# Two attention layers on eight images: layer 1's weighted sum by seven block products for six images, squares on two queues, steps ordered anew

## The chip, the cores and the metric

The kernel runs on one core of a Trainium2 chip. A core has TensorE (PE, with its weight loads shown as PEld), VectorE (DVE), ScalarE (ACT), GpSimd (POOL) and the queue engine SyncE (SP). Each engine works through its own queue in order. The metric is the device time in microseconds, the median of three runs.

## The reference

The input x is 8 images of 32 x 32 positions with 256 channels, all float32. So an image has 1024 tokens. Layer 0 is attention with four heads, layer 1 a gated attention with 32-wide keys.

```python
# layer 0, for each image b and head h
qkv = x @ W_qkv                      # q, k, v of 256 channels a head
atten = softmax(q @ k.T * 256**-0.5)
res = atten @ v
x1 = concat(res over heads) @ W_out + b_out + x

# layer 1
f, g, h = x1 @ Wf + bf, x1 @ Wg + bg, x1 @ Wh + bh
b = softmax(g @ f.T)                 # over the tokens of f
out = gamma * (b @ h) + x1
```

The softmax is over 1024 tokens. The division by the sum of exponentials can stand after the product with the values, because the sum belongs to the row of the output.

## The kernel before

**Steps.** The program is a list of steps. In layer 0 a step is one image, one head and one of two blocks of 512 query tokens. In layer 1 a step is one image and one block. For images 1 to 6 the list holds, in this order, heads 0 and 1 of the image, both blocks of layer 1 of the image before, and then heads 2 and 3. I name the steps of such an image 00, 01, 10, 11 (head, block), l0, l1, 20, 21, 30, 31. In the last image layer 1 of image 6 comes after all heads, and layer 1 of image 7 forms the end.

**What a step issues.** The loop over the steps at the end of the program collects tasks of several steps: the scores of this step, the block sums and value products of the step before, the last third of those products, the output projection and the queries of the next head. Each task gets a number (`put(tasks, *at)`), and the tasks are issued in the order of these numbers. TensorE, VectorE and ScalarE keep exactly this order (`manual_schedule`); the queues of SyncE and GpSimd are ordered by the framework.

**Seven products.** Large products are done on 2 x 2 blocks with seven products in place of eight (`seven`, line 253, `product` on line 271, whose matmuls all stand on line 273). One operand needs four sums of blocks beforehand (`sum_a`, `sum_b`). The function gives three tasks. Task one runs products 1 and 6, task two runs 5, 7 and 2, and task three runs 3 and 4; between them ScalarE copies partial results out of PSUM and VectorE adds them (line 290). Product 6 is the first that needs two dependent sums of blocks. Score banks are named psz, psy, psx; those of the value product have `_y`, of the output projection `_o`, of the queries `_q`.

**Layer 0.** Exponentials p (line 600) of a step are 128 x 8 x 512. The step after makes the block sums of p (line 638, tile ss), adds up all exponentials over the tokens in the free direction (lines 645 and 649, tile rs), and GpSimd adds over the partitions (PARTITION_ALL_REDUCE, line 651). The row of sums goes through DRAM to become columns (tile st), is inverted (line 667) and spread again over all partitions (tile invb). VectorE multiplies the projected output by it (line 725), and GpSimd's queue adds it to x1T by an accumulating DMA (line 728). The sums of the queries (tile qs) are on line 579.

**Layer 1.** f and g are made in one 128-row product and moved to four row groups (`queries_apart`, lines 804 and 816). The scores run four at a time on 32 rows (line 845), and ScalarE writes their exponentials (line 854, tile s). `values` makes gamma * (x1 @ Wh + bh) with 16 matmuls (line 518) and VectorE's line 828. `row_products` then runs, for each block, 4 x 8 matmuls of 257 columns (line 933, tile pa; column 257 is one, so it gives the sum of the exponentials), a reciprocal of it (line 941), and one instruction that multiplies and adds to x1 (line 943).

**Transposes.** x and x1 are turned between token rows and channel rows by DMAs of 32 x 32 squares and VectorE transposes within squares (`squares`, line 396, and line 418). All these DMAs are on SyncE's queue: 224 for x0T and 256 for x1.

Of the kernel before, what the change touches and what calls it, by code (L numbers as in the profile page):

```python
# [20 lines left out]
def kernel(  # L21
# [67 lines left out]
    FAR = 2.0**64  # L89
# [289 lines left out]
    xT_of, x1T_of, xblocks, vblocks = {}, {}, {}, {}  # L379
# [16 lines left out]
    def squares(dst, src, swap):  # L396

        Q = 32  # L400

        def move(a, c):
            for q in range(P // Q):
                to, rows_v = dst(), src()
                if swap:
                    nc.sync.dma_start(
                        to[ts(q, Q), :, c, ts(a, Q)], rows_v[ts(a, Q), c, :, ts(q, Q)]
                    )
                else:
                    nc.sync.dma_start(  # L410
                        to[ts(q, Q), c, :, ts(a, Q)], rows_v[ts(a, Q), :, c, ts(q, Q)]
                    )

        def piece(k):
            to = dst()
            n = to.shape[1] * to.shape[2] // 4
            flat = to.rearrange("p u v i -> p (u v) i")[:, ts(k, n), :]
            nc.vector.transpose(flat, flat)

        return (  # L420
            [partial(move, a, c) for a in range(P // Q) for c in range(CC)],
            [partial(piece, k) for k in range(4)],
        )
# [37 lines left out]
    def value_sums(b):  # L461

        made = {}

        def piece(i):
            if i == 0:
                r = rows[b]
                t = tile_of("xt", [P, 4, NT // 2, P], f"xt_{b}")
                blocks = [r[:, ts(j, NT // 2), ts(c, P)] for j in range(2) for c in range(CC)]
                sums = [t[:, k] for k in range(4)]  # L470
                made["l"] = sum_b(sums, *blocks)
                vblocks[b] = b_operands(blocks, sums)
            made["l"][i]()

        return [partial(piece, i) for i in range(4)]
# [58 lines left out]


    class Layer0:
# [82 lines left out]
        def sums(self, blk):  # L619
# [4 lines left out]
            made = {}  # L624

            def start():
                half = NT // 2
                p = self.p[blk]
                blocks = [p[:, ts(j, half), ts(e, HB)] for e in range(2) for j in range(2)]
                t = tile_of("ss", [P, 2, half, HB], f"ss_{n}")  # L630
                sums = [t[:, 1], t[:, 0], blocks[2], t[:, 0]]
                self.pblocks[blk] = a_operands(blocks, sums)
                made["t"], made["l"] = t, sum_a(sums, *blocks)

            def piece(i):
                if i == 0:
                    start()
                made["l"][i]()
# [8 lines left out]
            def last():  # L647
                r = made["r"]
                tt(r[:, 0, :], r[:, 0, :], r[:, 1, :], ALU.add)
                self.total[blk] = t = tile_of("rb", [P, NB], f"rb_{n}")  # L650
                nc.gpsimd.partition_all_reduce(  # L651
                    t, r.rearrange("p e i -> p (e i)"), P, bass_isa.ReduceOp.add
                )
                line = tile_of("line", [1, NB], f"line_{n}")
                nc.sync.dma_start(line, t[0:1, :])
                self.r[blk] = st = tile_of("st", [P, HT], f"st_{n}")
                with nc.allow_non_contiguous_dma(reason="a row of sums turns into columns"):
                    nc.sync.dma_start(st, line.rearrange("o (p t) -> p (o t)", p=P))

            adds = [partial(add, k) for k in range(1, NT // 2)]  # L660
            return [partial(piece, i) for i in range(4)], adds + [last]

        def invert(self, blk):
# [4 lines left out]
            if blk in self.rb:  # L668
                return
            line = tile_of("line", [1, NB], f"inv_{self.name}_{blk}")  # L670
            with nc.allow_non_contiguous_dma(reason="columns turn into a row"):
                nc.sync.dma_start(line.rearrange("o (p t) -> p (o t)", p=P), inv)
            self.rb[blk] = t = tile_of("invb", [P, NB], f"invb_{self.name}_{blk}")
            nc.sync.dma_start(t, line[0].partition_broadcast(P))
# [6 lines left out]
        def products(self, blk):  # L681


            def out(c, e):
                if blk not in self.y:
                    self.y[blk] = tile_of("y", [P, CC, NB], f"y_{self.name}_{blk}")
                return self.y[blk][:, c, ts(e, HB)].unsqueeze(1)

            return seven(
                f"y_{self.name}_{blk}", HB, 1,  # L690
                lambda number: [
                    (0, vblocks[self.b][number][:, j, :], self.pblocks[blk][number][:, j, :])
                    for j in range(NT // 2)
                ],
                {
                    "11": partial(out, 0, 0), "12": partial(out, 1, 0),
                    "21": partial(out, 0, 1), "22": partial(out, 1, 1),
                },
                NARROW,
            )  # L700
# [42 lines left out]
    class Layer1:  # L743
        scale = 1.0

        def __init__(self, b, direct=0):

            self.b, self.name, self.direct = b, f"{b}_l1", direct
            self.s = {}
            self.fg, self.v = None, None  # L750

# [23 lines left out]
        def queries_apart(self, tag=None):  # L775
# [7 lines left out]
            def task():  # L783
                fg = self.fg_tile()
                self.f, self.g = fg[:, 0, :], fg[:, 1, :]
                if tag is None:
# [33 lines left out]
        def values(self, last="psm"):  # L820
            def start():
                if self.v is None:
# [5 lines left out]
                lambda t2, pm: nc.vector.scalar_tensor_tensor(  # L828
                    self.v[:, 2 * t2 : 2 * t2 + 2, :C], pm, gamma_sb,
                    bh_sb.unsqueeze(1).broadcast_to([P, 2, C]), ALU.mult, ALU.add,  # L830
# [40 lines left out]
        def products(self, blk):  # L871
            return row_products(self, blk, rows1)

# [118 lines left out]
    steps, adds, exps = [], {}, {}  # L992

    for b in range(B):
        units = [Layer0(b, h) for h in range(HEADS)]
        if b > 0:
            units.insert(behind(b), Layer1(b - 1, NBLK))
        steps += [(u, blk) for u in units for blk in range(NBLK)]
# [9 lines left out]
    first_sums = value_sums(0)  # L1008
# [10 lines left out]
    for i, (a, blk) in enumerate(steps):  # L1019
        l0 = isinstance(a, Layer0)  # L1020
        one, two, nxt = step(i - 1), step(i - 2), step(i + 1)
        places = []

        def put(tasks, *at):
# [3 lines left out]
        if l0:  # L1028
            tasks, exps[i] = a.scores(blk)
            put(tasks, 0, 2, 4, 6, 8, 10)  # L1030
            put(exps[i][:2], 5.1, 6.1)
        else:
            tasks, _ = a.scores(blk)
            put(tasks, *((0.5, 2.4) if blk == 0 else (0.5, 2)))
        if is_l0(two):
            u, k = two
            put(u.products_of[k][2:], 1 if l0 else 0)
            if nxt is None:
                put([partial(u.invert_all, k)], 2.2)
            put([partial(u.invert, k)], 3.4 if l0 else 2.7)  # L1040
            ysums, tasks, adds[i] = u.project(k)
            put(ysums, *((1.1, 1.2, 1.3, 3.3) if l0 else (1.1, 1.2, 1.3, 2.5) if blk == 0 else
                         (0.6, 0.7, 0.8, 0.9)))
            put(tasks, *((3, 5.5, 7) if l0 else (4.5, 6, 7.2) if blk == 0 else
                         (3, 5, 7) if nxt else (1.9, 3.1, 4.1)))
            if nxt is None:
                put(adds[i], 4.2)
        if i - 1 in exps:
            put(exps[i - 1][2:], *((0.9, 0.91) if l0 else (0.1, 0.2)))
        if i - 1 in adds:  # L1050
            put(adds[i - 1], 0.5 if l0 or blk == 1 else 2.3)
        if is_l0(one):
            u, k = one
            sums, keys = u.sums(k)
            u.products_of[k] = u.products(k)
            put(sums, *((2.1, 3.2 if is_l0(two) else 2.4, 4.2, 5.6) if l0 else (0.8, 2.2, 3.5, 6.1)))
            put(keys, *((6.3, 6.6, 7.6, 8.7) if l0 else (6.3, 7.6, 8.3, 8.7)))
            put(u.products_of[k][:2], *((5, 9) if l0 else (4, 5)))
        elif one is not None:
            put(one[0].products(one[1]), *((3, 5, 7, 9) if l0 else (1, 4, 6, 8) if nxt else (1, 3, 4, 8.5)))  # L1060
        if i == 0:
            put(fold[0], 3.1, 3.2, 6.4, 6.5, 8.6)
            put(first_sums[:2], 8.4, 9.4)
        if i == 1:
            put(first_sums[2:], 1.4, 3.4)
            put(fold[1], 0.5, 0.6, 2.4, 2.6, 5.6)
            put(fold[2], 7.2, 7.3, 7.9, 9.2, 9.5)
            put([partial(nc.vector.tensor_scalar, bh_sb, bh_sb, gamma_sb, None, ALU.mult)], 8.5)

        if l0 and blk == 0:  # L1070
            put(a.query_sums(1), 3.5, 4.3, 4.4, 5.3)
        if is_l0(nxt) and blk == NBLK - 1:
            put(nxt[0].queries(), *((2.5, 4.5, 6.5) if not l0 else
                                    (1.5, 2.5, 4.5) if is_l0(two) else (0.5, 2.5, 5.5)))
            put(nxt[0].query_sums(0), *((6.7, 6.9, 7.3, 7.6) if not l0 else
                                        (5.4, 6.4, 7.2, 7.4) if is_l0(two) else (6.4, 7.2, 7.3, 7.4)))

        if l0 and a.h == 0 and blk == 1:
            put(residual(a.b), 5.3, 7.3)
        if l0 and a.h == 0 and blk == 1 and a.b > 0:  # L1080
            put(value_sums(a.b), 1.4, 2.4, 3.4, 4.4)
        if l0 and a.h == 1 and blk == 0 and a.b + 1 < B:
            load_x(a.b + 1)
        if is_l0(nxt) and nxt[0].h == 2 and nxt[1] == 0 and nxt[0].b + 1 < B:
            moves, turned = turn_rows(nxt[0].b + 1)
            put(moves[:4], 1, 2.5, 4, 5.5)
        if l0 and a.h == 2 and a.b + 1 < B:
            if blk == 0:
                put(moves[4:], 0.5, 1.5, 2.5, 3.5)
                put(turned, 6.4, 7.4, 8.4, 9.4)  # L1090
            else:
                put(key_sums(a.b + 1), 0.5, 0.6, 6.4, 7.4)

        if l0 and a.b > 0 and a.h == behind(a.b) - 1:
            if blk == 0:
                moves, turned1 = turn_back(a.b - 1)
                put(moves[:4], 3, 4.5, 6, 7.5)
            else:
                put(moves[4:], 4, 5.5, 7, 8.5)
                tasks, moves = nxt[0].queries_apart()  # L1100
                put(tasks, 1.5)
                put(moves, 1.6, 1.7, 1.8, 1.9)
        if not l0 and blk == 0:
            put(a.values("ps"), 0.9, 1, 2.3, 3, 6.5)
            put(turned1, 2.5, 2.9, 4.2, 5.1)
# [152 lines left out]
```

## Time and profile before

| | |
|---|---|
| median of 3 runs | 2305.72 us (2305.56 to 2306.0) |
| profiled execution | 2305.9 us, span of its instructions 2304.0 us |
| TensorE busy | 2293.2 us |
| VectorE busy | 1508.4 us |
| ScalarE busy | 756.9 us |
| GpSimd busy | 340.9 us |
| granted TensorE clock | 1.000 |

The profile is of one execution. A group is a line of the program with its engine, operation, tiles (output <- inputs), shape and count; then busy microseconds, mean nanoseconds of one, and the idle time of the engine just before. In the waits, a line says who waited for whom, in microseconds in total, how often, and the longest. In a timeline, the first number is the start in microseconds from the start of the span, the second is the duration; neighbouring equal instructions are merged (x4 means four). Matmul ends are modelled, so two neighbours overlap in the record, and the distance of starts is the real pace. A float32 matmul instruction shows as two records.

### The profile page before, as it was taken

To read this page: it belongs to the slowest core of one execution; us is meant where nothing else is said; L and a number is where in the kernel's file an instruction comes from. 1 tells how busy PE (TensorE), PEld (TensorE's weight loads), DVE (VectorE), ACT (ScalarE), POOL (GpSimd) and SP (SyncE) were. 2 spreads that over 40 slices of the span, in tenths; PEclk is the share of its full clock that TensorE was granted. 3 is DMA by queue.
4 is the path that set the end of the run, shared out by engine and by line. 5 is a ranking of instruction groups with operands and counts; after the bars stand their busy time and mean duration, and the time that the engine had idled before them with its cause. 6 is when DMAs were issued, how large, how long until landed. Compare 5 with 4: busy or idle time off the path is not lost.

```text
span 2304.0 us, 27262 instructions
## 1 busy us (share of the span) xinstructions
PE 2293.2 (100%) x10220; PEld 1887.2 (82%) x10220; DVE 1508.4 (65%) x2666; ACT 756.9 (33%) x1294; POOL 340.9 (15%) x243
## 2 busy tenths in 40 slices
PE   9999999999999999999999999999999999999999
PEld 7888888788887888788887888878888788888887
DVE  6776676476665766656766666656676557776663
ACT  3333333233332333323333233322333233333322
POOL 3111112011120112101121011210112101111211
PEclk9999999999999999999999999999999999999999
DMA  5111122301222113221132101321113211121222
GB/s 137 33 28 28 28 37 44 74 15 28 47 45 63 18 25 57 38 60 19 28 54 44 53 19 29 58 43 50 19 28 58 46 29 19 28 46 28 40 40 61
DMA packets 200925, 94.83 MB, mean 41 GB/s; under 512 B 165968, under 2 KB 170192, under 8 KB 200784
## 3 DMA queue, kind: packets, MB, share of 16 engines
q1 hardware_dynamic: 180176, 54.06, 11.2%
q0 software_dynamic: 20608, 38.94, 9.6%
q8 instruction: 83, 1.36, 0.2%
q14 instruction: 58, 0.48, 0.1%
HBM read 29.76 MB, written 8.65 MB: 17 GB/s over the span
## 4 chain that ended last, share of the span: by engine, by line
PE 98%; DVE 1%; DMA 1%; ACT 1%; issue 0%; ACTq 0%; SPq 0%
PE psz_y L273 14%; PE psy_y L273 14%; PE psz L273 14%; PE psy L273 14%; PE pa_l L933 10%; PE psz_o L273 7%; PE psx L273 5%; PE psx_y L273 5%; PE psz_q L273 3%; PE psy_q L273 3%; PE pr_v_l L518 3%; PE ps_l L845 1%; PE psx_q L273 1%; PE psx_o L273 1%; PE pm_fg L795 1%; DMA invb<-inv 0%
## 5 line engine op out<-in xcount | busy, mean ns | idle before, releaser
L651 POOL PARTITION_ALL_REDUCE rb<-rs x64 | 206.5, 3226 | 1448.8 <-issue 1153.4
L600 ACT ACTIVATE p<-p 128x1024 f32<-128x1024 f32 x256 | 263.9, 1056 | 74.5 <-DVE p L290 74.3
L273 PE MATMUL psz<-q,xs 128*128 128x256 f32 x1024 | 264.6, 381 | 0.0
L273 PE MATMUL psy<-qs,xs 128*128 128x256 f32 x1024 | 263.0, 379 | 1.2 <-DVE qs L579 1.2
L273 PE MATMUL psy_y<-p,xt 128*128 128x256 f32 x1024 | 241.9, 379 | 0.0
L933 PE MATMUL pa_l<-v_l,s_l 128*128 128x257 f32 x1024 | 232.1, 381 | 0.0
L273 PEld LDWEIGHTS psz<-q,xs 128*128 128x128 f32 x1024 | 192.9, 190 | 47.2 <-issue 19.1
L933 PEld LDWEIGHTS pa_l<-v_l,s_l 128*128 128x128 f32 x1024 | 193.7, 190 | 34.3 <-issue 6.8
L273 PEld LDWEIGHTS psy<-qs,xs 128*128 128x128 f32 x1024 | 193.3, 190 | 29.2 <-DVE qs L579 1.6
L296 ACT COPY e<-psz 128x512 f32<-128x512 f32 x128 | 75.1, 586 | 431.6 <-PE psz L273 431.6
L273 PEld LDWEIGHTS psy_y<-p,xt 128*128 128x128 f32 x1024 | 194.6, 190 | 26.4
L290 DVE TENSOR_TENSOR p<-psy,v 128x512 f32<-128x512 f32 x128 | 88.0, 688 | 87.7 <-ACT v L304 44.4
L728 POOL DMA_DIRECT2D x1T<-o x64 | 77.4, 1210 | 407.5 <-DVE o L725 354.2
L273 PE MATMUL psz<-q,x0T 128*128 128x256 f32 x512 | 131.4, 379 | 0.0
L273 PE MATMUL psx<-q,x0T 128*128 128x256 f32 x512 | 131.4, 379 | 0.0
L273 PE MATMUL psy<-qs,x0T 128*128 128x256 f32 x512 | 131.4, 379 | 0.0
L273 PE MATMUL psx_y<-p,x 128*128 128x256 f32 x512 | 121.0, 379 | 0.0
L273 PE MATMUL psz_y<-ss,x 128*128 128x256 f32 x512 | 121.0, 379 | 0.0
L273 PE MATMUL psy_y<-ss,xt 128*128 128x256 f32 x512 | 121.0, 379 | 0.0
L273 PE MATMUL psz_y<-p,x 128*128 128x256 f32 x512 | 120.9, 379 | 0.0
L273 PE MATMUL psz_y<-ss,xt 128*128 128x256 f32 x512 | 120.9, 379 | 0.0
L273 PEld LDWEIGHTS psz_y<-p,x 128*128 128x128 f32 x512 | 97.3, 190 | 20.9 <-PE psz_q L273 4.3
(153 smaller groups left out, 3700.5 us busy)
## 6 DMA issues: line engine op xcount, KB each, us to landing
x1T<-o POOLq DMA_DIRECT2D x64, 512.0 KB, 5.0
invb<-inv SPq DMA_DIRECT2D x63, 256.0 KB, 4.0
x<-x1T SPq DMA_DIRECT2D x256, 32.0 KB, 2.0
out_dram<-x SPq DMA_DIRECT2D x15, 512.0 KB
x<-in_x_dram SPq DMA_DIRECT2D x14, 512.0 KB, 4.4
x0T<-x SPq DMA_DIRECT2D x224, 32.0 KB, 2.0
fg<-v_l POOLq DMA_DIRECT2D x56, 64.0 KB, 2.0
w<-in_L_conv_W_qkv_dram POOLq DMA_DIRECT2D x36, 32.0 KB, 3.3
```

Source lines behind the costliest of these rows:

```text
L273: nc.tensor.matmul(banks[k][:, ts(i, w)], lhsT=lhsT, rhs=rhs, start=first and n == 0, stop=True, skip_group_check=True,)
L290: nc.vector.tensor_tensor(dst, shaped(banks[k]), shaped(other), ALU.add)
L296: nc.scalar.copy(scratch("e"), banks["z"])
L518: nc.tensor.matmul(pm[:, ts(j, C)], lhsT=src()[:, c, ts(2 * t2 + j, P)], rhs=w()[:, c, :], start=(c == 0), stop=(c == CC - 1),)
L600: exp(both, both)
L651: nc.gpsimd.partition_all_reduce(t, r.rearrange("p e i -> p (e i)"), P, bass_isa.ReduceOp.add)
L728: nc.gpsimd.dma_start(x1T_of[self.b][:, :, ts(blk, NB)], o, accum_op=ALU.add)
L795: nc.tensor.matmul(pm[ts(k, half)], lhsT=w[:, c, :], rhs=x1T_of[b][:, c, ts(k, NB)], start=(c == 0), stop=(c == CC - 1),)
L845: nc.tensor.matmul(pm, lhsT=self.f[ts(r, CK), ts(j0 + r, P)], rhs=self.g[ts(r, CK), ts(blk, NB)], start=True, stop=True,)
L933: nc.tensor.matmul(pm[:, : C + 1], lhsT=p[:, j, ts(ti, P)], rhs=v[:, j, : C + 1], start=(j == 0), stop=(j == NT - 1),)
```

## The change

For images 0 to 5 layer 1 works with x1 itself as the values: first y = x1 * exponentials by `seven` (like layer 0), then y @ Wh, and the bias is added at the end. For the seven products, the two column halves of an exponential block of 512 queries are added to each other before the division, and the result of the projection is scaled by token. The new `weigh` adds up the exponentials by token, makes the ratio of the sums of the first 256 queries to those of the other 256 on chip, and multiplies the second half by it, so that one inverse per pair of halves is enough. Gamma goes into W_h and b_h once at the start. For images 1 to 6 the steps of layer 1 now stand before and after step 20: 00, 01, 10, 11, l0, 20, l1, 21, 30, 31. Each of the ten has its own table of numbers. Squares go to SyncE and GpSimd's queue in turn. Images 6 and 7 keep the old layer 1, and the first and the last image keep the old numbers. The checks on the sums use a limit of 2**60 in place of 2**64.

```diff
-    FAR = 2.0**64
+    FAR = 2.0**60
...
             for q in range(P // Q):
                 to, rows_v = dst(), src()
+                queue = nc.sync if q % 2 else nc.gpsimd
                 if swap:
-                    nc.sync.dma_start(
+                    queue.dma_start(
...
+    def block_sums(u, blk):
...
+        def weigh(self, blk):
+            def add(k):
+                s = self.s[blk]
+                if k == 1:
+                    made["r"] = tile_of("rs", [P, NB], f"rs_{n}")
+                tt(made["r"], s[:, 0, :] if k == 1 else made["r"], s[:, k, :], ALU.add)
+            def total():
+                made["t"], self.r[blk] = sums_to_columns(
+                    made["r"], n, "o (t p) -> p (o t)"
+                )
+            def ratio():
+                t = made["t"]
+                made["i"] = i = tile_of("rs", [P, HB], f"ratio_{n}")
+                nc.vector.reciprocal(i, t[:, HB:])
+                tt(i, i, t[:, :HB], ALU.mult)
+            def scale(k):
+                q = NT // 2
+                s = self.s[blk][:, ts(k, q), HB:]
+                tt(s, s, made["i"].unsqueeze(1).broadcast_to([P, q, HB]), ALU.mult)
+            adds = [partial(add, k) for k in range(1, NT)]
+            return adds + [total], [ratio] + [partial(scale, k) for k in range(2)]
+        def block_products(self, blk):
+            return block_products(self, blk, v1blocks)
+        def project(self, blk):
+            def start():
+                made["o"] = o = tile_of("m0", [P, HT, C], f"out_{self.name}_{blk}")
+                nc.vector.tensor_tensor(
+                    o, rows1[self.b][:, ts(blk, HT), :],
+                    bh_sb.unsqueeze(1).broadcast_to([P, HT, C]), ALU.add,
+                )
...
+                nc.vector.reciprocal(made["i"], self.r[blk])
+            def task(t2):
+                pm = tile_of("psm", [P, NB], f"po_{self.name}_{blk}_{t2}")
...
+                for j in range(2):
+                    for c in range(CC):
+                        nc.tensor.matmul(
+                            pm[:, ts(j, C)],
+                            lhsT=y[:, c, ts(2 * t2 + j, P)],
+                            rhs=wh_sb[:, c, :],
...
+                for j in range(2):
+                    o = made["o"][:, 2 * t2 + j, :]
+                    nc.vector.scalar_tensor_tensor(
+                        o, pm[:, ts(j, C)], made["i"][:, j : j + 1], o, ALU.mult, ALU.add
+                    )
...
+    PLACES = {
+        "01": {
+            "scores": (1.002, 2.1, 3.947, 5.411, 7.573, 9.985),
...
+            "sums": (2.449, 2.486, 5.297, 6.018),
...
+            "product": (5.304, 8.43),
...
+            "values": (0.829, 2.259, 3.023, 5.954),
...
+        "11": {
+            "scores": (-0.672, 1.477, 4.474, 6.259, 7.097, 10.847),
...
+            "scale": (1.665,),
+            "sums": (2.545, 4.269, 4.535, 5.335),
...
+            "product": (5.08, 10.947),
...
+        "l0": {
+            "scores": (0.5, 1.055),
...
+            "project": (2.615, 5.534, 7.719),
...
+            "sums": (0.76, 2.2, 3.511, 4.1),
...
+            "product": (3.276, 6.328),
+            "last product": (0.151,),
...
+            "weigh": (5.794, 6.122, 6.222, 6.822, 6.887, 7.022, 7.122, 7.96),
+            "queries": (0.97, 4.53, 6.5),
+            "first queries": (7.07, 7.27, 7.67, 7.97),
...
+        "20": {
+            "scores": (-0.784, 2.171, 3.846, 5.393, 7.167, 10.522),
...
+            "project": (3.119, 4.823, 6.435),
+            "scale": (1.93,),
+            "sums": (4.4, 4.828, 5.29, 6.103),
...
+            "product": (5.654, 9.47),
+            "last product": (0.539,),
...
+            "ratio": (2.411, 3.484, 3.8),
+            "own values": (2.287, 2.348, 2.448, 6.883),
...
+        "l1": {
+            "scores": (2.066, 5.177),
...
+            "sums": (0.699, 2.619, 3.162, 4.118),
...
+            "product": (3.866, 5.664),
+            "last product": (-0.843,),
...
+            "weigh": (7.615, 8.227, 8.327, 8.538, 9.027, 9.127, 9.361, 10.228),
...
-            units.insert(behind(b), Layer1(b - 1, NBLK))
-        steps += [(u, blk) for u in units for blk in range(NBLK)]
+        order = [(u, blk) for u in units for blk in range(NBLK)]
+        if 0 < b < B - 1:
+            u = Layer1(b - 1, NBLK, True)
+            order[NBLK * behind(b) : NBLK * behind(b)] = [(u, 0)]
+            order[NBLK * behind(b) + 2 : NBLK * behind(b) + 2] = [(u, 1)]
...
+        own = PLACES[f"{a.h if l0 else 'l'}{blk}"] if mid else {}
+        def put(name, tasks, *at):
+            at = own.get(name, at)
...
-            put([partial(nc.vector.tensor_scalar, bh_sb, bh_sb, gamma_sb, None, ALU.mult)], 8.5)
+            put("gamma", [partial(nc.vector.tensor_scalar, t, t, gamma_sb, None, ALU.mult)
+                 for t in (bh_sb, wh_sb)], 8.5, 8.6)
```

In a table, "weigh" are the seven additions of exponentials and the release of the all-reduce, "ratio" the ratio and the two scalings, "own values" the four sums of x1's blocks, "sums" the four block sums of the exponentials of the step before, "product" tasks one and two of its value product, "last product" task three of the one before that, "first queries" the four sums of the next head's queries.

## The prediction

> **What bounds the kernel now.** I read the page's busy times and its chain, then the groups by line, then the waits, then the timeline of VectorE and TensorE in one middle image. Busy times and chain:
>
> ```profile
> PE 2293.2 (100%) x10220; PEld 1887.2 (82%) x10220; DVE 1508.4 (65%) x2666; ACT 756.9 (33%) x1294; POOL 340.9 (15%) x243
> PE 98%; DVE 1%; DMA 1%; ACT 1%; issue 0%; ACTq 0%; SPq 0%
> ```
>
> TensorE is never idle to speak of. The change can gain only by taking matmuls away, and any wait it puts in front of TensorE is paid in full. Groups by line, and one answer of the waits:
>
> ```profile
> L933 PE MATMUL pa_l<-v_l,s_l 128*128 128x257 f32 x1024 | 232.1, 381 | 0.0
> L518 PE MATMUL pr_v_l<-wh_sb,x1T 128*128 128x256 f32 x256 | 60.9, 386 | 0.1
> L645 DVE TENSOR_TENSOR rs<-rs,ss 128x512 f32<-128x512 f32 x128 | 87.7, 685 | 1.3
> L638 DVE TENSOR_TENSOR ss<-ss,p 128x1024 f32<-128x1024 f32 x64 | 78.2, 1221 | 1.3
> L679 DVE RECIPROCAL invb<-rb 128x512 f32<-128x512 f32 x1 | 3.3, 3344 | 0.0
> PE psy L273 <- DVE qs L579: 1.2, 1, 1.2
> ```
>
> One f32 matmul instruction shows as two records. The 381 ns is overlapped, so the pitch is read from the chain in order of time:
>
> ```profile
> 413.97 3.47 PE pa_l L933 x16
> ```
>
> 3.47/16 = 0.217 us a record; 256-wide matmuls run at 0.216 in the same timeline, 512-wide ones at 0.429. The last line of the groups' fence says that in the whole run TensorE waited once, 1.2 us, for sums of queries.
>
> What VectorE takes per instruction must also be read as a pitch (start to start), on the timeline of VectorE, and the delay behind TensorE by setting it against TensorE's:
>
> ```profile
> 741.21 1.22 DVE L638 TENSOR_TENSOR ss<-p 128x1024 f32<-128x1024 f32 x1
> 742.45 1.23 DVE L638 TENSOR_TENSOR ss<-ss,p 128x1024 f32<-128x1024 f32 x1
> 743.60 0.68 DVE L290 TENSOR_TENSOR q<-psy_q,v_q 128x512 f32<-128x512 f32 x1
> 744.20 0.68 DVE L290 TENSOR_TENSOR q<-psx_q,e_q 128x512 f32<-128x512 f32 x1
> ...
> 753.09 0.42 DVE L579 TENSOR_TENSOR q<-q 128x256 f32<-128x256 f32 x1
> 753.54 0.42 DVE L579 TENSOR_TENSOR qs<-q 128x256 f32<-128x256 f32 x1
> ```
> ```profile
> 747.95 1.02 PE L273 MATMUL psy_q<-x0T,wt 128*128 128x512 f32 x2
> 748.81 1.03 PE L273 MATMUL psz<-q,x0T 128*128 128x256 f32 x4
> ```
> ```profile
> 749.01 0.69 DVE L290 TENSOR_TENSOR q<-psy_q,e_q 128x512 f32<-128x512 f32 x1 [0.17 <-PE psy_q L273]
> ```
>
> A 1024-wide addition holds the queue 1.15 us (1.24 when the next needs its result), a 512-wide one 0.60 (0.71), a 256-wide one 0.34 (0.46). psy_q's last record gives way to psz at 748.81, and VectorE starts on psy_q at 749.01: 0.20 us.
>
> **What the Trainium skill says.** "SBUF — State Buffer", section "Who interferes with whom": a VectorE instruction with two SBUF inputs and a GpSimd instruction that reads SBUF exclude each other, and whichever starts first blocks the other. The trace agrees. All seven L725 multiplications (two SBUF inputs) that met the all-reduce took 2.86 us instead of 1.22:
>
> ```profile
> 682.38 2.86 DVE L725 TENSOR_TENSOR o<-o,invb 128x1024 f32<-128x1024 f32 x1
> ```
> ```profile
> 681.93 3.23 POOL L651 PARTITION_ALL_REDUCE rb<-rs  x1 [15.62 <-issue]
> ```
>
> It started 0.45 us into the all-reduce and lost 1.65, so the block lasts to 2.1 us after the all-reduce's start. "TensorE: Matmul & The Clock Gate", section "Part 1: The HAM clock gate": after an idle window of about 3.4 us TensorE falls to half clock until a busy one. No stage of this run shows it after the start; I keep it for the upper bound.
>
> **The change, part by part.** TensorE. Removed for six images: 384 instructions of pa_l = 768 records x 0.217 = 166.7 us, and 96 of pr_v_l = 192 x 0.216 = 41.5. Added: 7 products x 4 x 2 blocks = 56 instructions an image, 336 in all = 672 x 0.216 = 145.2, and 96 of po_l = 41.5. Net 96 records fewer, **-21.5 us**, 3.6 an image. All of it lies on the bound.
>
> VectorE, per image, added: 14 additions of probabilities (0.685) 9.6, 2 reciprocals of 256 at half the 3.34 of L679 3.4, 2 ratio products 0.8, 4 scalings 4.9, 8 block sums 9.7, 4 own-value sums 2.7, 8 additions of y 3.4, 2 of x1 and bias 2.4, 8 into the output 3.9, 2 short reciprocals 0.3: 41.1. Removed: 4 of L828 3.0, 8 reciprocals 1.3, 8 of L943 3.9. Net +33 us on 185 busy of a 284 us image, now 218 of 280, or 78%. That fits on average, so what matters is where it stands. ScalarE gets 6 copies of 0.37 an image, at 33% load: nothing on the path.
>
> Queues. 240 of the 480 squares go to GpSimd's queue; the same shape of L216 costs about 0.58 us there, 9.2 for an image's 16. They stand two all-reduces ahead of layer 1's first; what waits behind them is one all-reduce a time, needed half a step (over 10 us) later. Twelve more all-reduces (3.23) and their line and column DMAs feed the output, which nobody on the path awaits; only the ratio does. SP loses 216 issues net. Scaling W_h by gamma once and the new FAR are one short instruction under TensorE's first work. I cost all this at nothing; if the cover failed, a late ratio of 1 us would cost 6 in all.
>
> The order. In the changed program's queues I looked at each TensorE instruction that waits for VectorE and added up what stands between it and the TensorE result that starts the chain. (Score products are 4 records, 0.864 us; y products 8, 1.728; o products 2, 0.432.)
>
> - A, end of step l0, six times. The last query product ends; TensorE has o (0.864) and a score product (0.864), then score product 6 needs the second query sum. VectorE: 0.20, addition 0.60, three additions of probabilities 0.71+0.71+0.60, query sum 0.34, a fourth addition 0.60, sums 0.46+0.42 = 4.6. Late by **2.9-3.0**. That fourth addition also releases the all-reduce, just before the last sum (two SBUF inputs, about 0.25 us into it). If it is blocked to 2.1 us, **4.8**.
> - B, step 20. From the end of y of (head 1, block 1) TensorE has 46 records, 9.9 us, to layer 1's product 6, which needs the second block sum. VectorE in that stretch: y and its sums 0.34+0.10+0.46+0.46+0.34+0.34 = 2.0, scaling of o 1.15, score additions 4 x 0.60, value sums 3 x 0.60, reciprocal 1.7 and ratio 0.34, two scalings 2.3, first block sum 1.15, three of 0.34 1.0, second block sum 1.22 = 15.1, with 0.2 and 0.1 of delays 15.4. Late by **5.4**.
> - C, step l1, product 6 of head 2: VectorE 0.2+0.34+1.15+1.24+1.22+0.1 against ps_l and one y product, 2.8: **1.4**.
> - D, E, F: the same sum for layer 1's block 1 (11.9 against 11.6), step 01 (value sums, 4.6 against 3.5) and step 11 (4.9 against 4.3): **0.4 + 1.1 + 0.6**.
>
> Together 13.7 us an image with the block, 11.8 without. I take the block, since all seven meetings show it: 6 x 13.7 = 82. The waits don't absorb each other: each is counted from a TensorE result that the wait before it has moved along.
>
> Sum on the profiled execution: span 2304.0 - 21.5 + 82 = 2364.5, and 1.9 around it (2305.9) makes 2366.4; the median of the runs is 0.2 below that: **2366 us**.
>
> **Rivals.** (1) The new work is hidden and the kernel is faster: 2305.7 - 21.5 = 2284. For it: no wait of this kind before, VectorE at 78%. It decides at B: all waits would have to stay under 3.6 us an image, and B alone is 5.4. It would need the ratio's chain to be several us shorter than L679 and L638 make it. (2) Waits of about half: if reciprocal and dependent pitches are overstated, and A is not blocked, some 7 an image: 2305.7 - 21.5 + 42 = 2326. (3) TensorE's clock drops in A and B, both longer than 3.4 us: half speed for one window loses 1.7 us, twice an image, 20 us: 2386; with late all-reduces about 2392. Against: no drop in the trace of before, and the window must lie wholly inside the wait. (4) The matmul count doesn't fall: excluded, since the built program holds 48 fewer instructions.
>
> **How the numbers follow.** Sum as given 0.60, own range 2348 (no block, small waits gone) to 2380; half the waits 0.18; clock or queues 0.13; hidden 0.06; gain and waits cancel 0.03. What a measurement here can tell is about 0.2%. So faster 0.06, same 0.03, slower 0.91. The range of 8 in 10 reaches part of the way into (2) and (3): 2334 to 2390.
>
> **What would show it.** Right: TensorE waits on VectorE in the list of waits, six each of psy<-qs about 3-5 us, psy_y_l<-ss about 5.4, psy_y<-ss about 1.4; TensorE's busy time about 21 lower; the reciprocal at 1.7. Wrong: those waits absent or under 1 us, a reciprocal far below 1.7, or waits by transfers (x1T, fg, invb) in their place.

## The result and the profile after

The changed kernel takes 2395.3 us (median of 4 runs, 2394.0 to 2395.4) against 2305.7 us, a ratio of 1.0387 with a 95% interval of 1.0369 to 1.0405. The direction was right; the time lies 29 us above the forecast and 5 us above the top of the range. The profiled execution has a span of 2393.6 us, 89.6 more than before.

The page of the changed kernel, busy times and the chain by engine:

```profile
PE 2305.6 (96%) x10124; PEld 1888.5 (79%) x10124; DVE 1702.9 (71%) x2871; ACT 771.2 (32%) x1330; POOL 518.4 (22%) x489
PE 82%; DVE 12%; issue 4%; POOL 1%; DMA 0%; SPq 0%; ACT 0%; DVEq 0%; ACTq 0%
core 0: 2393.6 us, clock 0.986
```

TensorE has 96 records fewer (10124), yet it is busy for 12 us longer. VectorE now holds 12% of the chain that ended last; it held 1%. The last line is the core's span and its mean granted TensorE clock, which was 1.000 before.

The list of waits of TensorE in the changed kernel (total us, number, longest us):

```profile
PE psy_y_l L273 <- DVE ss_l L574: 33.3, 12, 5.3
PE psy L273 <- DVE qs L642: 30.3, 7, 4.9
PE psy_y L273 <- DVE ss L574: 9.7, 12, 1.1
PE psy_y L273 <- DVE xts L474: 6.1, 6, 1.0
```

These are B with D, A, C with F, and E of the prediction. TensorE's timeline in one middle image of the changed kernel (start, length, what, and in brackets the idle time before it with its releaser) shows A and B, and something more:

```profile
993.78 1.03 PE L273 MATMUL psz<-q,x0T 128*128 128x256 f32 x4
999.66 2.04 PE L273 MATMUL psy<-qs,xs 128*128 128x256 f32 x4 [4.85 <-DVE qs L642]
1001.50 3.34 PE L273 MATMUL psz_y<-ss,x 128*128 128x256 f32 x8
1004.67 1.89 PE L273 MATMUL psy_y<-p,xts 128*128 128x256 f32 x8
...
1021.75 3.52 PE L273 MATMUL psy_y_l<-ss_l,x1s 128*128 128x256 f32 x8 [5.26 <-DVE ss_l L574]
```

The four records behind A take 2.04 us where four take 1.03 otherwise, and the eight after them 3.34 instead of 1.89; the eight behind B take 3.52. The same matmuls are done at half speed. The windows view of the changed kernel, cut at the 3.41 us steps on which the clock changes in this trace (stretch; length, busy us and records of each engine, granted clock, DMA), for wait A of an earlier image:

```profile
693.80:697.21 3.41, 1.77 (x9) 1.21 (x7) 3.34 (x7) 0.59 (x1) 0.00 (x0) 1.00 0.00 0
697.21:700.62 3.41, 0.20 (x1) 0.23 (x2) 3.38 (x5) 0.00 (x0) 2.90 (x1) 1.00 0.00 0
700.62:704.04 3.42, 3.42 (x9) 2.71 (x9) 0.66 (x2) 0.59 (x1) 0.37 (x1) 0.50 0.10 6
```

TensorE is busy for 0.20 us of the second window, and the third is granted 0.50: nine records in it where a full one has 17 or 18.

VectorE in the first image shown, and beside it GpSimd:

```profile
997.16 2.35 DVE L642 TENSOR_TENSOR qs<-q 128x256 f32<-128x256 f32 x1
...
1012.06 1.75 DVE L918 RECIPROCAL ratio_l<-rb_l 128x256 f32<-128x256 f32 x1
...
1014.78 2.35 DVE L924 TENSOR_TENSOR s_l<-s_l,ratio_l 128x1024 f32<-128x1024 f32 x2
...
1020.39 1.21 DVE L574 TENSOR_TENSOR ss_l<-ss_l,s_l 128x1024 f32<-128x1024 f32 x1
```
```profile
996.95 3.27 POOL L541 PARTITION_ALL_REDUCE rb_l<-rs_l  x1 [7.28 <-DVE rs_l L908]
```

The second query sum, started 0.21 us into the all-reduce, takes 2.35 us instead of the 0.42 of its neighbours; the reciprocal takes 1.75.

Where the 89.6 us come from. I take the starts of TensorE's records and count what the interval to the next one has above the record's own pitch (0.216, or 0.429 at 512 wide): over 0.45 us it is a wait, from 0.15 to 0.45 a record at half speed. The waits sum to 84.8 us (2.2 before), the slow records to 30.3 us in 130 records (4.1 us in 13 before). So -21.5 (96 records fewer) + 82.6 + 26.2 = 87.3. Some 2 us are left over; waits under 0.45 us are not in this count.

### The profile page after: what moved, and what is told of

The parts are those of the page before. It is cut to its first block, busy times and chain, and to the rows that moved or that the text cites. A ratio compares the mean times of both kernels' runs of the same rounds, so it can differ in the third digit from the quotient of the medians.

```text
span 2393.6 us, 27533 instructions
## 1 busy us (share of the span) xinstructions
PE 2305.6 (96%) x10124; PEld 1888.5 (79%) x10124; DVE 1702.9 (71%) x2871; ACT 771.2 (32%) x1330; POOL 518.4 (22%) x489
## 4 chain that ended last, share of the span: by engine, by line
PE 82%; DVE 12%; issue 4%; POOL 1%; DMA 0%; SPq 0%; ACT 0%; DVEq 0%; ACTq 0%
PE psy_y L273 13%; PE psy L273 13%; PE psz L273 12%; PE psz_y L273 12%; PE psz_o L273 5%; PE psx L273 4%; PE psx_y L273 4%; PE psy_y_l L273 3%; PE psz_q L273 2%; PE psy_q L273 2%; PE pa_l L1032 2%; DVE ss L574 2%; PE po_l L954 2%; PE psz_y_l L273 2%; DVE p L290 1%
## 5 line engine op out<-in xcount | busy, mean ns | idle before, releaser
L273 PE MATMUL psy<-qs,xs 128*128 128x256 f32 x1024 | 268.9, 386 | 30.3 <-DVE qs L642 30.3
L273 PE MATMUL psy_y<-p,xts 128*128 128x256 f32 x1024 | 242.3, 379 | 0.0
L273 PEld LDWEIGHTS psy_y<-p,xts 128*128 128x128 f32 x1024 | 195.0, 190 | 26.8
L304 ACT COPY v<-psz 128x512 f32<-128x512 f32 x128 | 75.0, 586 | 237.3 <-PE psz L273 237.3
L290 DVE TENSOR_TENSOR p<-psy,v 128x512 f32<-128x512 f32 x128 | 88.1, 689 | 74.7 <-PE psy L273 69.5
L273 PE MATMUL psy_y<-ss,xts 128*128 128x256 f32 x512 | 122.3, 382 | 15.8 <-DVE ss L574 9.7
L273 PE MATMUL psz_y<-ss,x 128*128 128x256 f32 x512 | 128.5, 396 | 0.0
L273 PEld LDWEIGHTS psy_y<-ss,xts 128*128 128x128 f32 x512 | 95.8, 190 | 34.8 <-PE psz_y L273 13.5
L273 PE MATMUL psz_y<-ss,xts 128*128 128x256 f32 x512 | 121.0, 379 | 0.0
L273 PEld LDWEIGHTS psz_y<-ss,x 128*128 128x128 f32 x512 | 102.4, 201 | 20.4 <-issue 4.9
```

The lines of the kernel that those rows point to most:

```text
L273: nc.tensor.matmul(banks[k][:, ts(i, w)], lhsT=lhsT, rhs=rhs, start=first and n == 0, stop=True, skip_group_check=True,)
L290: nc.vector.tensor_tensor(dst, shaped(banks[k]), shaped(other), ALU.add)
L304: nc.scalar.copy(scratch("v"), banks["z"])
```

## The experiments

All times are set against runs of the kernel before on the same chip, 2305.5 to 2305.9 us there. A and B are such excesses, per image (0.16 us above the bracketed idle time, since a record lasts 0.38 us and the pitch is 0.216); slow records are over the whole run.

| kernel | us | ratio to before, 95% | A, us | B, us | slow records: number, us |
|---|---|---|---|---|---|
| changed | 2395.3 | 1.0369 to 1.0405 | 5.02 | 5.42 | 130, 30.3 |
| query sums first | 2359.8 | 1.0219 to 1.0254 | 0.56 | 5.63 | 74, 17.7 |
| fourth addition late | 2366.0 | 1.0244 to 1.0278 | 2.61 | 5.42 | 60, 14.5 |
| product late | 2404.8 | 1.0411 to 1.0446 | 5.02 | moved, 5.60 | 161, 36.8 |
| first and third together | 2361.6 | 1.0227 to 1.0261 | 0.56 | moved, 5.80 | 78, 18.5 |
| squares on one queue | 2395.7 | 1.0374 to 1.0409 | 5.01 | 5.42 | 123, 29.4 |
| no scaling | 2364.7 | 1.0245 to 1.0279 | 5.01 | 3.15 | 56, 12.6 |
| kept busy in B | 2384.2 | 1.0325 to 1.0357 | 5.02 | 1.54 | 82, 20.2 |
| new order, first | 2311.6 | 1.0018 to 1.0039 | 0.56 | 1.75 | 12, 3.1 |
| new order, second | 2293.8 | 0.9935 to 0.9962 | none | none | 6, 1.8 |

**Query sums first.**

```diff
 "l0": {
-    "first queries": (7.07, 7.27, 7.67, 7.97),
+    "first queries": (6.6, 6.61, 6.62, 6.63),
```

> The four query sums of head 2 are put ahead of the last five additions of probabilities in step l0, so that only the query's own addition stands between the last query product and the second sum; nothing is left out. Theory (wait A is VectorE's queue, and each of the waits A and B is followed by half clock that costs about 2.2 us): psy<-qs falls from 5.0 to under 0.5 us and the slow matmul records behind it vanish, those behind B stay: -(4.6 + 2.2) x 6 = -41, about 2354. Rival (the slow records are not caused by the wait, or move elsewhere): -4.6 x 6 = -28, about 2367. Rival (VectorE is simply behind, and the wait turns up later in the step): nothing won, 2390 to 2395. B (psy_y_l<-ss_l) stays at 5.3 to 5.4 in all of them.

Measured 2359.8. TensorE in this kernel, same place in the same image:

```profile
981.09 1.03 PE L273 MATMUL psz<-q,x0T 128*128 128x256 f32 x4
982.51 1.10 PE L273 MATMUL psy<-qs,xs 128*128 128x256 f32 x4 [0.40 <-DVE qs L642]
983.45 1.89 PE L273 MATMUL psz_y<-ss,x 128*128 128x256 f32 x8
```

The eight records behind it take 1.89 us again. A is shorter by 4.46 x 6 = 26.8 us, the slow records by 12.6, and B grew by 0.21 x 6 = 1.3; the sum, -38.1, stands against -36.2 of span. So A was the order of VectorE's queue alone, and its slow records went with it. The time, 35.5 us under the changed kernel's, lies between the theory's -41 and the first rival's -28; what rules that rival out is the clock, which falls to half six times here, each time behind a B, where the changed kernel has twelve such falls. The second rival (nothing won) is out by the time.

**Fourth addition late.**

```diff
 "l0": {
-    "weigh": (5.794, 6.122, 6.222, 6.822, 6.887, 7.022, 7.122, 7.96),
+    "weigh": (5.794, 6.122, 6.222, 6.822, 6.887, 7.022, 7.68, 7.96),
```

> Only the last addition of probabilities of step l0, which releases the all-reduce, is moved behind the second query sum; nothing is left out. Theory (the all-reduce blocks that sum for 1.9 us): without the block and without the addition's 0.6 us A falls from 5.0 to about 2.5; a wait of 2.5 us is shorter than the window of 3.4 us, so no slow records behind A: -(2.5 + 2.2) x 6 = -28, about 2367. Rival (no block, the long sum has another cause): A falls by the addition's 0.6 alone to 4.4 and the slow records stay: about 2391. Rival (clock drops behind any wait of some us): A 2.5 with slow records, about 2380.

Measured 2366.0. A is 2.61: it lost 2.41, of which the addition's own pitch is 0.60, so the all-reduce's block cost 1.8. The block itself hasn't gone; it falls on the fourth sum, for which nobody is in a hurry. VectorE in this kernel:

```profile
990.57 2.10 DVE L642 TENSOR_TENSOR qs<-q,qs 128x256 f32<-128x256 f32 x1
```

TensorE's wait in the same image is [2.46], with no slow record behind it. In one image of the six there were some, though. The windows of two images of this kernel, the one with and one without:

```profile
691.24:694.65 3.41, 0.96 (x5) 0.54 (x4) 3.27 (x7) 0.59 (x1) 0.00 (x0) 1.00 0.00 0
694.65:698.06 3.41, 3.41 (x10) 2.70 (x9) 2.79 (x4) 0.59 (x1) 3.15 (x1) 0.50 0.02 5
...
984.78:988.20 3.42, 2.30 (x10) 1.50 (x8) 3.35 (x7) 0.59 (x1) 0.00 (x0) 1.00 0.01 2
988.20:991.61 3.41, 2.08 (x10) 1.88 (x11) 3.34 (x7) 0.59 (x1) 1.47 (x1) 1.00 0.02 5
991.61:995.02 3.41, 3.41 (x18) 3.00 (x17) 2.27 (x5) 0.03 (x1) 1.77 (x1) 1.00 0.00 1
```

The same wait of 2.5 us costs half speed where it lies in one window, which leaves TensorE 0.96 us of work there, and nothing where a window's edge divides it (2.30 and 2.08). My expectation, no half clock under a wait of 3.4 us, was near in its time (2367) by luck: its reason is wrong, and five of the six waits escaped half speed because an edge divided them.

**Product late.**

```diff
 "20": {
-    "sums": (4.4, 4.828, 5.29, 6.103),
+    "sums": (4.4, 4.828, 5.29, 10.65),
...
-    "product": (5.654, 9.47),
+    "product": (10.6, 10.7),
```

> Layer 1's first products of step 20 (numbers 1, 6, and then 5, 7, 2) are issued behind the last score products of that step, and the fourth block sum behind them; nothing is left out. Theory (B is the distance of the second block sum from the products that need it): TensorE has 3.0 to 4.7 us more of other products ahead of product 6, so psy_y_l<-ss_l falls from 5.4 to 0.7 to 2.4 and its slow records vanish: -(3.0 to 4.7 + 2.2) x 6 = -31 to -41, about 2354 to 2364; A stays at 5.0. Rival (VectorE is behind by 5 us anyway, and TensorE then waits for the additions that free its PSUM banks or for the next query sums): the same waiting under other names, 2385 to 2395.

Measured 2404.8. The rival has the mechanism right, but its range (2385 to 2395) ends 10 us lower. TensorE's waits in this kernel:

```profile
PE psz_o L273 <- DVE o L290: 32.8, 7, 5.4
...
PE psy_y_l L273 <- DVE ss_l L574: 1.7, 6, 0.3
```

B is gone by its name and comes back, 0.2 us longer, at an earlier product: the last products of `project` need the PSUM bank that VectorE empties by L290, and that addition stands behind the same value sums, reciprocal, ratio and scalings. B is therefore not the distance of one product from its operand but VectorE's backlog at this point of the step. Putting other matmuls ahead of the product doesn't help while those matmuls wait for the same queue. Of the 9.5 us by which this kernel is slower than the changed one, 6.5 are in slow records: its clock stays at half for two windows behind all twelve waits, in the changed kernel behind seven.

**Both.** The edits of the first and the third.

> The edits of the first and the third run together. Theory (A and B are independent waits, each paid with its own clock loss): the gains add, -72 to -82, about 2313 to 2323, with C to F (3.5 us an image, 21 in all) left. Rival (VectorE's backlog): the second gain is partly lost, 2340 to 2355.

Measured 2361.6, near neither figure: the third edit's gain isn't partly but wholly lost, since the first edit alone gives 2359.8.

**Squares on one queue.**

```diff
-                queue = nc.sync if q % 2 else nc.gpsimd
+                queue = nc.sync
```

> The changed kernel with all squares issued by SyncE again, as before the change; the order and the products stay, nothing is left out. Theory (the division over two queues is on no path): no change, 2395, within 0.2%, and the same waits A 5.0 and B 5.4. Rival (POOL's 16 issues of 9.3 us an image hold up the all-reduces that the ratio or the scaling of o needs): faster by 5 us or more, with A or B shorter. Rival (SyncE's queue was the tighter one): slower, with waits on transfers of x or x0T in the list.

Measured 2395.7, with A and B as they were. The division over the queues is worth nothing here, as costed.

**No scaling.**

```diff
-            return adds + [total], [ratio] + [partial(scale, k) for k in range(2)]
+            return adds + [total], [ratio] + [lambda: None for k in range(2)]
```

> The changed kernel without the two scalings of the second half's probabilities by the ratio (2.35 us of VectorE a block, twice an image); the ratio itself is still made, and this part of the computation is left out. Theory (B is the length of VectorE's queue ahead of the second block sum, one for one): B falls from 5.4 by 2.3 to 3.1 us, which is under 3.4, so its slow records vanish too: -(2.3 + 2.2) x 6 = -27, about 2368. Rival (half clock follows at 3.1 as well): -14, about 2381. Rival (the queue would only wait elsewhere, at the product's own probabilities): under 5 us won, 2390 or more. A stays at 5.0 with its slow records.

Measured 2364.7. B falls by 2.27 for 2.35 us of VectorE's work, one for one, which is what a backlog does. The wait left, 3.15 us, is followed by no slow record in any of the six images. That is no proof of my reason (under 3.4 us): an edge divides the wait in all six and leaves TensorE 1.63 us of work or more in every window. What a wait of this length does inside one window, this run doesn't show. The windows of this kernel about three of its waits A:

```profile
688.41:691.82 3.41, 1.38 (x7) 0.87 (x5) 3.34 (x7) 0.59 (x1) 0.00 (x0) 1.00 0.00 0
691.82:695.23 3.41, 0.59 (x2) 0.54 (x3) 3.38 (x5) 0.00 (x0) 3.27 (x1) 0.50 0.00 0
...
1275.50:1278.91 3.41, 1.44 (x7) 0.94 (x5) 3.34 (x7) 0.59 (x1) 0.00 (x0) 1.00 0.00 0
1278.91:1282.33 3.42, 0.54 (x3) 0.52 (x4) 3.39 (x6) 0.00 (x0) 3.24 (x1) 1.00 0.00 0
1282.33:1285.74 3.41, 3.41 (x10) 2.70 (x9) 0.32 (x1) 0.59 (x1) 0.03 (x1) 0.50 0.08 1
...
1569.05:1572.46 3.41, 1.33 (x7) 0.82 (x5) 3.34 (x7) 0.59 (x1) 0.00 (x0) 1.00 0.00 0
1572.46:1575.87 3.41, 0.64 (x2) 0.58 (x3) 3.38 (x5) 0.00 (x0) 3.27 (x1) 0.50 0.00 0
1575.87:1579.29 3.42, 3.42 (x10) 2.71 (x9) 0.21 (x1) 0.59 (x1) 0.00 (x0) 0.50 0.08 1
```

A window with 1.44 us of work is followed by full speed, those with 1.38 and 1.33 us by half. The limit lies between 1.38 and 1.44 us, at about 40% of a window.

**Kept busy in B.**

```diff
             for k, number in (("z", 1), ("y", 6)):
                 bank(k)
+                for i, lhsT, rhs in matmuls(1)[:1] * (warm if k == "z" else 0):
+                    nc.tensor.matmul(
+                        banks[k][:, ts(i, w)], lhsT=lhsT, rhs=rhs,
+                        start=True, stop=True, skip_group_check=True,
+                    )
...
-            return block_products(self, blk, v1blocks)
+            return block_products(self, blk, v1blocks, 0 if blk else 9)
```

> The changed kernel with nine more matmuls (128x256, 0.432 us each, 3.9 us) ahead of layer 1's first product in step 20 of the middle images; they write the product's own PSUM bank, which the product then overwrites. VectorE's work and its lateness stay as they are; TensorE only has something to do in 3.9 of the 5.4 us of wait B. Theory (half clock follows from an idle TensorE, and costs 2.2 us behind each B): the wait shrinks to about 1.5 us, its slow records vanish, and although TensorE has 23 us more work the kernel gets faster by 6 x 2.2 = 13: about 2382. Rival (the slow records belong to the place or to the load, not to idleness): no gain, 2395, with as many slow records as before.

Measured 2384.2. TensorE in this kernel:

```profile
1010.74 4.05 PE L296 MATMUL psz_y_l<-s_l,x 128*128 128x256 f32 x18
1014.62 1.89 PE L273 MATMUL psz_y_l<-s_l,x 128*128 128x256 f32 x8
1017.89 1.97 PE L273 MATMUL psy_y_l<-ss_l,x1s 128*128 128x256 f32 x8 [1.38 <-DVE ss_l L579]
1019.69 0.59 PE L273 MATMUL psz_o<-y,wo 128*128 128x256 f32 x2
```

The first line is the work that was added, the third has 1.97 us where it had 3.52. With 23.3 us more of matmuls the kernel is 11.1 us faster. The lateness of the operand is the same, so half speed is the price of TensorE's idleness and is paid on top of the wait; the slow records fell by 10.1 us.

**New order, first.** New places in the tables of the middle images, chosen so that by the durations of these traces each operand is ready when its product comes. In three of the tables the additions of `keys` stand ahead of a block sum that they read, so those row sums are made from other data; the work is of the same length. The line that decided:

```diff
 "l0": {
-    "scores": (0.5, 1.055),
+    "scores": (0.473, 0.474),
...
 "l1": {
-    "scores": (2.066, 5.177),
+    "scores": (-0.563, -0.542),
```

> The changed kernel with other places in the tables of the middle images: the query sums of head 2 ahead of the last additions of probabilities, layer 1's first products of step 20 later, and VectorE's sums and scalings spread over the neighbouring steps; the same instructions, nothing left out. Theory (the loss is the order alone, and 21.5 us of matmuls are really saved): A, C, E, F and D under 0.6 us each, B about 1.7, no half clock: 2393.6 - 82.6 - 26.2 + 6 x 2.3 = 2299 of span, about 2300 in all, under the kernel before. Rival (VectorE at 78% can't be arranged without waits): the waits turn up under other names, 2320 to 2360.

Measured 2311.6, 12 us above the theory. A, C, D, E, F and B came out as expected; the rest is new. TensorE in this kernel, and below it a line of its weight loads' waits:

```profile
999.96 3.42 PE L868 MATMUL ps_l<-fg 32*128 32x512 f32 x16
```
```profile
PEld ps_l L868 <- ACT s_l L877: 10.5, 25, 0.7
```

Layer 1's two score tasks of a block now stand directly behind each other. Each takes four PSUM banks, the program has six for them, and TensorE waits for ScalarE's exponentials to empty them. Alone, a task takes 1.07 us; the pair takes 3.35. That is 3.35 - 2 x 1.07 = 1.2 us a pair, twelve pairs, some 14 us.

**New order, second.** Places found anew, the score tasks apart and the additions of `keys` behind their sums again. The core of the diff:

```diff
 "l0": {
-    "scores": (0.5, 1.055),
+    "scores": (1.27, 4.388),
...
-    "weigh": (5.794, 6.122, 6.222, 6.822, 6.887, 7.022, 7.122, 7.96),
+    "weigh": (4.591, 5.232, 5.233, 6.129, 6.131, 6.132, 6.63, 9.739),
-    "queries": (0.97, 4.53, 6.5),
-    "first queries": (7.07, 7.27, 7.67, 7.97),
+    "queries": (1.353, 4.362, 4.363),
+    "first queries": (4.377, 4.378, 4.651, 6.591),
...
 "20": {
-    "scores": (-0.784, 2.171, 3.846, 5.393, 7.167, 10.522),
+    "scores": (-2.946, 1.425, 4.439, 5.181, 5.182, 9.18),
...
-    "scale": (1.93,),
-    "sums": (4.4, 4.828, 5.29, 6.103),
+    "scale": (0.971,),
+    "sums": (3.997, 4.038, 6.229, 7.229),
...
-    "product": (5.654, 9.47),
+    "product": (7.054, 10.738),
...
-    "own values": (2.287, 2.348, 2.448, 6.883),
+    "own values": (0.685, 3.156, 3.998, 6.219),
```

> The changed kernel with a second set of places in the tables of the middle images: the same instructions, nothing left out. Query sums of head 2 stand ahead of the last additions of probabilities in step l0; layer 1's first products in step 20 stand behind more score products; its four score matmuls per task stand apart again, so that TensorE does not wait for ScalarE to empty six PSUM banks; VectorE's sums are spread over the neighbouring steps. Theory (the whole loss is waits made by the order, plus the half clock that follows long ones; the 21.5 us of matmuls are really saved): no wait of TensorE on VectorE above 0.6 us in the middle images, 1 us an image in all: 2305.5 - 21.5 + 6 = about 2290, faster than the kernel before (between 2284 and 2297). Rival (VectorE at 78% and ScalarE leave no order without waits; they return under other names): 2305 or more.

Measured 2293.8, faster than the kernel before by 12 us. The page of this kernel, stretches of TensorE in two middle images, and the longest waits of its matmuls in the middle images:

```profile
PE 2280.9 (99%) x10124; PEld 1867.8 (81%) x10124; DVE 1693.3 (74%) x2871; ACT 771.0 (34%) x1330; POOL 518.4 (23%) x489
```
```profile
667.53 1.97 PE L868 MATMUL ps_l<-fg 32*128 32x512 f32 x8
...
975.22 1.89 PE L273 MATMUL psz_y_l<-s_l,x 128*128 128x256 f32 x8
976.94 1.89 PE L273 MATMUL psy_y_l<-ss_l,x1s 128*128 128x256 f32 x8
...
989.99 1.14 PE L868 MATMUL ps_l<-fg 32*128 32x512 f32 x8
```
```profile
PE psy_q L273 <- DVE q L290: 2.0, 6, 0.3
```

The same instructions as in the changed kernel, 10124 records on TensorE and 2871 on VectorE, take 101 us less of span. Nothing in the new arithmetic made the change slow; the places did. Of the 21.5 us of matmuls, some 10 are still lost. By the starts of TensorE's records, 3 of them are the six waits above (0.49 us each), and 5 lie in six of layer 1's score tasks, which take 1.9 us instead of 1.07 (the first line of the stretches is one).

## Why the prediction was wrong

**TensorE, -21.5 us.** Right by the count of records; the second new order shows that more than half of it can be had. The sign named for it, TensorE's busy time about 21 lower, didn't come: records at half speed last longer, and busy time rose by 12.

**VectorE, +33 us an image.** Right: 1702.9 - 1508.4 us over six images is 32.4.

**The waits, 82 us.** Right in place, number and size. Predicted and measured per image: A 4.8 and 5.0, B 5.4 and 5.4, C 1.4 and 1.3, D 0.4 and 0.45, E 1.1 and 1.2, F 0.6 and 0.65. Six images of these make 84; the count above has 82.6, since D lies at its limit of 0.45. That they don't absorb each other held as well.

**The all-reduce's block.** Right: 2.35 us for a sum of 0.42, and 1.8 us of A by the run with the fourth addition late. Here, too, the block ends about 2.1 us after the all-reduce's start (997.16 + 2.35 - 0.42 - 996.95), not at its end at 3.27.

**Reciprocal.** Right: 1.7 foreseen, 1.75 measured.

**Work costed at nothing.** For the squares' division over two queues the run with one queue shows it. The scaling of W_h, the new FAR and the twelve output all-reduces were not tried apart. No wait in the list points at them, and the second new order contains them all.

**The clock: the step that failed.** The main sum had no term for it. It stood as rival (3), "half speed for one window loses 1.7 us, twice an image, 20 us: 2386", with the words "Against: no drop in the trace of before, and the window must lie wholly inside the wait", and shared a chance of 0.13. Both reasons were bad. The trace before has no wait of TensorE for another engine above 1.4 us, so it could show no drop. And the window needn't lie inside the wait: what counts is that TensorE works for less than about 1.4 us of one window of 3.41. A is 4.9 us idle; even when an edge halves it, 2.45 us fall in each window and leave 0.96. By this condition half speed was certain behind all twelve waits, and the trace has it behind all twelve. The loss was 26.2 us, 2.2 a wait instead of 1.7, since the clock stayed at half through a second window behind seven of them. With this term the sum would have been 2366 + 26 = 2392, against 2395 measured.

The Trainium skill, "TensorE: Matmul & The Clock Gate", pointed to it. Its section "Part 1: The HAM clock gate" says that the window runs freely and doesn't start with the kernel; the 3.41 us grid of these traces agrees. Its section "HAM oscillation — how this bites in real kernels" shows a loop in which waits for transfers, 3 to 5 us long, bring half clock back in every single round; here waits of 5.0 and 5.4 us do, twelve of twelve, and the prediction used only the first of the two. Where the page has an idle window as the condition, as the prediction had, these traces show up to 1.38 us of work in the window, 40% of it, to be little enough.

Rival (1), the new work hidden, fell at B: its 5.4 us came in full. Rival (2), waits of about half, fell too: the reciprocal took 1.75 us, A's sum was blocked, and no wait was half as long as foreseen.

## What to carry to other kernels

When an engine that bounds a kernel gets a new wait of several microseconds, add a second term to the wait: what its clock loses behind it, and settle that term by how much work the wait can leave in one of the clock's windows, not by whether the old trace shows it. A wait for a backlogged queue isn't cured by moving the one instruction that waits, for its neighbours wait on the same queue; take work out from ahead of the operand. A faster algorithm and the order it is issued in are two changes: here the first is worth a gain and the second cost 100 us.

## What was not expected of the hardware

The condition for half speed was sharp. I cut all eleven traces at the 3.41 us steps of their clocks, leaving out the first 20 us and the end. Half speed followed on 67 windows at full speed, and in each of them TensorE worked for 1.38 us or less. In every window that was followed by full speed it worked for 1.44 us or more. The way back was stricter: a window at half speed with 2.81 us of work or more was followed by full speed, one with 2.72 or less by a second window at half speed, so TensorE may idle for only about a fifth of it. Two such windows, each with the next, from the run with the fourth addition late:

```profile
418.17:421.58 3.41, 2.71 (x7) 2.18 (x8) 2.02 (x3) 0.00 (x0) 0.00 (x0) 0.50 0.00 0
421.58:425.00 3.42, 3.42 (x10) 2.66 (x9) 2.20 (x4) 0.37 (x1) 0.00 (x0) 0.50 0.00 0
...
715.13:718.54 3.41, 2.81 (x7) 2.27 (x8) 1.93 (x3) 0.00 (x0) 0.00 (x0) 0.50 0.00 0
718.54:721.96 3.42, 3.42 (x18) 3.00 (x17) 2.84 (x6) 1.49 (x3) 0.00 (x0) 1.00 0.00 0
```

Layer 1's score matmuls use 32 rows of the array each, and four of them that use different rows run side by side: the two records of four such instructions, eight in all, take 1.07 us, while one 512-wide matmul over all rows takes 0.86. Where the PSUM banks weren't free in time, in the first new order, part of this gain was lost: two such groups took 3.35 us.
